# Attention and experts in one kernel: order of the slot scatters, more tiles of the last batch in memory, a fixed first run, independent row scatters and spare banks for transposes

## The chip, the cores and the metric

The kernel runs on one core of a Trainium2 chip. The metric is the device time of one launch in microseconds, a median of several runs. The engines are TensorE (PE, with its weight load PEld), VectorE (DVE), ScalarE (ACT), GpSimd (POOL) and SyncE (SP), which only issues transfers here. Each has a queue of instructions in an order that is fixed when the kernel is built.

## The reference

Two layers with residual additions, on `x` of 4 batches x 1024 tokens x 1024 features and a context of 4 x 1024 x 256, all in float32. The second layer has 8 experts of width 3584, two for each token.

```python
def _L0_xattn_ref(p, k_v, W_k, b_k, ln_gamma, ln_beta):
    kv = k_v @ W_k.T + b_k
    out = jnp.einsum('bij,bjd->bid', p, kv)
    sim = jnp.einsum('bid,bjd->bij', out, kv) * scale
    mu = jnp.mean(sim, axis=-1, keepdims=True)
    var = jnp.var(sim, axis=-1, keepdims=True)
    sim = (sim - mu) * jax.lax.rsqrt(var + EPS) * ln_gamma + ln_beta
    return jax.nn.softmax(sim, axis=-1)

def _L0_ffn_ref(x, gate_w, w1, w2, w3):
    x_flat = x.reshape(-1, d)
    router_probs = jax.nn.softmax(x_flat @ gate_w, axis=-1)
    topk_w, topk_idx = jax.lax.top_k(router_probs, TOP_K)
    topk_w = topk_w / jnp.sum(topk_w, axis=-1, keepdims=True)
...
    h = jax.lax.ragged_dot(x_rep_sort, w1, group_sizes)
    h = jax.nn.silu(h) * jax.lax.ragged_dot(x_rep_sort, w3, group_sizes)
    out_sort = jax.lax.ragged_dot(h, w2, group_sizes)
...
    return jnp.einsum('tkd,tk->td', out_rep, topk_w).reshape(b, s, d)

x = x + _L0_xattn_ref(_layernorm(x), ctx_512, ...)
x = x + _L0_ffn_ref(_layernorm(x), ...)
```

## The kernel before

The kernel has two halves with a hand-over between them.

**Attention, 32 tiles of 128 tokens, 8 per batch.** `front(b)` (L226) prepares a batch: the context is transposed and projected to `kv`, each tile of tokens is loaded (`xt`), normalised (`pn`), transposed into `pT`, and `attend` multiplies with `kv`. `back(b, g)` (L318) then takes one tile: `sim` on PE; its sum of squares on ACT, written over `z`; a power on POOL (`power`, L198: two small operations); the scaling and the softmax on DVE and ACT, in place in `z`; the residual sum `x1`, which SP writes to the output; the layer norm `hn` (`normed`, L206, with one more power on POOL), which SP writes to a scratch tensor `h_d`; eight transposes of `hn`, and eight narrow matmuls for the gate, whose result DVE copies into `lg` (L363). The steps of `front(b + 1)` are put in between the tiles of `back(b, ...)`, so the last batch has none. Pool `wk` gives two buffers to each of `z`, `x1`, `hn` and `pn`, pool `big` two to `pT`.

**Routing.** After each group of four tiles (two groups of two at the end, `GROUPS`) `route` (L368) picks the two experts of each token and its slot in a table `id_d` with a region of `REG` rows for each expert. `put` (L452) scatters token number and weight into the slots: one indirect transfer on POOL for each tile and choice, 64 in all. After every tile two scatters are taken from the list `to_put` (L485), and what is left comes at the end (L500). They are declared independent of one another by the group "puts". The framework places each instruction on its engine's queue by a simulated readiness, program order deciding between those that are ready; an instruction can be pinned behind what was written before it on its engine with `keep_in_program_order`.

**The table of runs.** From the number of tokens of each expert, DVE computes on one partition which expert each run serves (`run_e`), where its slots start (`run_s`), its kind (`run_k`, one of 27 pairs of block count and width in `RUNS`) and how many runs there are (`run_n`), L523 to L584.

**Hand-over.** L926 to L931: `load_rows(first_slot(0))` reads the start of the first run from `run_s`, loads the slots' numbers (`load_ids`, a transfer of SP that waits for all slot scatters), clips them on DVE (`where_from`) and gathers five tiles of rows from `h_d` on POOL. `load_first` loads the first two weight tiles of the expert that `run_e` names. `tokens_in` (L747) transposes the rows into `x`: for each of five tiles, two groups of four transposes into a PSUM tile `pt` of pool `pst`, which has one buffer, and a copy on ACT or DVE.

**Experts.** A loop of two runs a turn (L933), each a `Switch` over the kinds. `run` (L821) works on one or two blocks of up to 564 tokens, with seven products in place of eight (factors are made on DVE). The first part of a block makes the hidden layer (matmuls L855), the second the output (L911). The order of PE is as written here. Small steps are taken from a list `late` between the matmuls: `tokens_out` (L793) transposes results back through `pt`, DVE adds them to the rows, weighted (L802), and after the last quarter POOL scatters each tile of rows to the output (L807); `tokens_in` with `rows_of_out` (L885) prepares the next block and gathers the output's rows. The last quarter of a run is left for the next run (`leftover`, L818), and after the loop for L944. `banks` (L663) takes PSUM for the products: one tile of pool `ps1` and three of pool `ps2`, each of two banks.

Of the kernel before, what the change touches and what calls it, by code (L numbers as in the profile page):

```python
# [9 lines left out]
F32 = mybir.dt.float32  # L10
I32 = mybir.dt.int32
AF = mybir.ActivationFunctionType
ALU = mybir.AluOpType
# [6 lines left out]
P = 128  # L20
N = 512
# [4 lines left out]
MOST = HOLD[-1]  # L26
# [3 lines left out]
TOP_K = 2  # L30
# [4 lines left out]
def kernel(  # L35
# [14 lines left out]
    nc = tc.nc  # L50
    B, S, D = x.shape
# [7 lines left out]
    NT = T // P  # L59
    KM = M // P  # L60
    MAXQ = -(-T // MOST)
    NRUN = (T * TOP_K + E * (MOST - 1)) // MOST
    TAB = 16
    REG = T + -(-(MOST + P) // P) * P
    NONE = 2 * T
# [37 lines left out]
    with ExitStack() as st:  # L103
# [210 lines left out]
                yield lambda h=h: attend(h)  # L314

        lgs = {}

        def back(b, g):  # L318

            row = ts(b * G + g, P)  # L320
            h, i = divmod(g, HG)
            oT, kvT, xt = oTs[b, h], kvTs[b], xts.pop((b, g))
            sim = ps_s.tile([P, J], F32, tag="sim", name="sim")
            for c in range(J // N):
                for d in range(KC):
                    nc.tensor.matmul(
                        sim[:, ts(c, N)], oT[:, d, ts(i, P)], kvT[:, d, ts(c, N)],
                        start=(d == 0), stop=(d == KC - 1),
                    )

            z = wk.tile([P, J], F32, tag="z", name="z")
            ss = sm.tile([P, 1], F32, tag="ss", name="ss")
            nc.scalar.activation(z, sim, AF.Square, accum_out=ss)
            r = power(ss, scale2 / J, SIM_EPS, "s")
            nc.vector.scalar_tensor_tensor(z, sim, r, ngam, ALU.mult, ALU.mult)
            nmax = sm.tile([P, 1], F32, tag="nmax", name="nmax")
            nc.vector.tensor_tensor_reduce(
                z, z, nbet, 1.0, BIG, ALU.add, ALU.min, accum_out=nmax
            )
            den = sm.tile([P, 1], F32, tag="den", name="den")  # L340
            nc.scalar.activation(z, z, AF.Exp, bias=nmax, scale=-1.0, accum_out=den)
            rden = sm.tile([P, 1], F32, tag="rden", name="rden")
            nc.vector.reciprocal(rden, den)
            x1 = wk.tile([P, D], F32, tag="x1", name="x1")
            nc.vector.scalar_tensor_tensor(x1, z, rden, xt, ALU.mult, ALU.add)
            nc.sync.dma_start(out=of[row, :], in_=x1)
            hn = wk.tile([P, D], F32, tag="hn", name="hn")
            normed(hn, x1, "h")
            nc.sync.dma_start(out=h_d[row, :], in_=hn)
            hT = wk.tile([P, KD, P], F32, tag="hT", name="hT")  # L350
            transposed(hT, hn)
            pm = ps_m.tile([P, N], F32, tag="pm", name="pm_g")
            for k in range(KD):
                nc.tensor.matmul(
                    pm[:, :E], hT[:, k, :], gw[:, k, :],
                    start=(k == 0), stop=(k == KD - 1),
                )
            t = b * G + g
            u = max(i for i, (t0, _) in enumerate(GROUPS) if t0 <= t)
            t0 = GROUPS[u][0]  # L360
            if t == t0:
                lgs[u] = wk.tile([P, RG, E], F32, tag="lg", name="lg")
            nc.vector.tensor_copy(lgs[u][:, t - t0, :], pm[:, :E])  # L363
# [4 lines left out]
        def route(u, lg, base):  # L368
# [83 lines left out]
            def put(t, k):  # L452
                to = nc.gpsimd.indirect_dma_start(
                    out=id_d,
                    out_offset=bass.IndirectOffsetOnAxis(ap=pos[:, k, t : t + 1], axis=0),
                    in_=tok[:, k, t, :],
                    in_offset=None,
                )


                if puts:
                    tc.declare_no_dep(to.ins, group="puts", reason="slots are disjoint")
                    for c in cleared:
                        tc.add_manual_dep(to.ins, c.ins.name, SYNC)
                tc.add_to_no_dep_group("puts", to.ins)
                puts.append(to)

            to_put.extend(
# [37 lines left out]
        def row(name, n=E):  # L506
            return tb.tile([1, n], F32, name=name)
# [17 lines left out]
        for j in range(MAXQ):  # L525
            nc.vector.scalar_tensor_tensor(
                nr, n_e, float(j * MOST), nr, ALU.is_gt, ALU.add
            )
        kind, hold = row("kind"), row("hold")
        nc.vector.memset(kind, 0.0)  # L530
        nc.vector.memset(hold, float(HOLD[0]))
# [61 lines left out]
    with ExitStack() as st:  # L593
# [28 lines left out]
        def weights(dst, wf, ex, k0, kn, c0):  # L622
            nc.sync.dma_start(
                out=dst[:, :kn, :],
                in_=wf[ds(ex, 1), :, k0 : k0 + kn, c0 : c0 + QW].rearrange(
                    "e p k m -> (e p) k m"
                ),
            )
# [62 lines left out]
        def expert(i):  # L691
            return nc.values_load(
                run_e[:, ds(i, 1)], engines=(ENG.SP,), min_val=0, max_val=E - 1
            )
# [16 lines left out]
            nc.vector.tensor_scalar(rd, ids[:, :, 0], T - 1, None, ALU.min)  # L711

        def gather(dst, src, rd, s, n):
            nc.gpsimd.indirect_dma_start(
                out=dst,
                out_offset=None,
                in_=src,
                in_offset=bass.IndirectOffsetOnAxis(ap=rd[:n, s : s + 1], axis=0),
            )
# [17 lines left out]
        def load_rows(s0):  # L737
            load_ids(ids0, s0)
            where_from(rd0, ids0)
            for s, r in enumerate(ROWS):  # L740
                gather(rows[s][:r, :], h_d, rd0, s, r)

        def load_first(i, j):

            weights(wts_in[j], (w1f, w3f)[j], expert(i), 0, KD, 0)

        def tokens_in(then=None):  # L747


            def step(s, h):  # L750
                r = ROWS[s]
                pt = pst.tile([P, 4, P], F32, tag="pt", name="pt_h")
                for k in range(HK):
                    nc.tensor.transpose(  # L754
                        pt[:, k, :r], rows[s][:r, ts(HK * h + k, P)], ident[:r, :r]
                    )
                dst = x[:, ds(HK * h, HK), ds(s * P, r)]
                if h % 2:
                    nc.vector.tensor_copy(dst, pt[:, :, :r])
                    if then is not None:  # L760
                        then(s)
                else:
                    nc.scalar.copy(dst, pt[:, :, :r])

            return [lambda s=s, h=h: step(s, h) for s in range(RT) for h in range(2)]
# [24 lines left out]
                p5=v[:, T1, :], p6=t2, p7=t[:, 1, :],  # L790
            )

        def tokens_out(ids, split, q, y):  # L793

            yv = y.rearrange("p (d c) -> p d c", d=2)

            def step(s, r):
                pt = pst.tile([P, 4, P], F32, tag="pt", name="pt_y")
                for d in range(2):
                    nc.tensor.transpose(pt[:r, d, :], yv[:, d, ds(s * P, r)], ident)  # L800
                part = rows[s][:r, ts(q, QW)]
                nc.vector.scalar_tensor_tensor(  # L802
                    part, pt[:r, 0:2, :].rearrange("p a b -> p (a b)"),
                    ids.bitcast(F32)[:r, s, 1:2], part, ALU.mult, ALU.add,
                )
                if q == DQ - 1:
                    nc.gpsimd.indirect_dma_start(  # L807
                        out=of,
                        out_offset=bass.IndirectOffsetOnAxis(ap=ids[:r, s, 0:1], axis=0),
                        in_=rows[s][:r, :],  # L810
                        in_offset=None,
                        bounds_check=T - 1,
                        oob_is_err=False,
                    )

            return [lambda s=s, r=r: step(s, r) for s, r in enumerate(split)]

        def leftover():  # L818
            return tokens_out(ids1, ROWS, DQ - 1, y1)

        def run(i, ex, s0, blocks, width):  # L821
            n = width // 2
# [10 lines left out]
            def take_ids():  # L833
# [3 lines left out]
                nc.vector.tensor_copy(rd, rd0)  # L837
                return ids, rd

            late = leftover()  # L840
            right = token_factors(n)
            for b in range(blocks):
# [41 lines left out]

                def rows_of_out(s):  # L885
                    if s < len(split):
                        gather(rows[s][: split[s], :], of, rd, s, split[s])

                late += tokens_in(rows_of_out)
                if not last:  # L890
# [1 line left out]
                for q in range(DQ):  # L892
                    pp = banks()
                    i2 = 0
                    for u, kn in enumerate(W2K):
# [7 lines left out]
                        if last and q == DQ - 1 and u == len(W2K) - 1:  # L903

                            assert j % WR == WR - 1 == 2
                            load_first(i + 1, 0)
                            load_first(i + 1, 1)
                            late.append(lambda: weight_sums(0, KD, False))
                        hid = [hidden_factors(g[:, i2 + k, :, :], n) for k in range(kn // 2)]
                        for at_m, (p, k) in enumerate(todo):  # L910
# [12 lines left out]
                    late += tokens_out(ids, split, q, y)  # L923
            assert not late

        load_rows(first_slot(0))  # L926
        load_first(0, 0)
        load_first(0, 1)
        for step in tokens_in():
            step()  # L930
        weight_sums(0, KD, False)  # L931
        n_run = nc.values_load(run_n, min_val=2, max_val=NRUN + NRUN % 2)
        with tc.For_i(0, n_run, 2) as i0:  # L933
# [5 lines left out]
            for i, ex, s0, kind, kinds in heads:  # L939
                for k in tc.Switch(kind, kinds):  # L940
                    if k < len(RUNS):
                        with tc.manual_schedule(engines={ENG.PE}):
                            run(i, ex, s0, *RUNS[k])
        for step in leftover():  # L944
            step()


# [26 lines left out]
```

## Time and profile before

| what | us |
|---|---|
| median of three runs | 8915.48 (8914.19 to 8917.11) |
| the profiled execution | 8914.97 |
| its span | 8913.3 |
| first matmul of the experts (L855) | 547.1 |
| last matmul of the experts (L911) ends | 8886.7 |
| mean granted PE clock | 0.988 |

The span runs from the first to the last instruction of one profiled execution. Attention takes about 500 us, routing of the last tiles and the hand-over some 45, the experts the rest. The costliest groups are all matmuls of the experts and their weight loads:

```profile
L855 PE MATMUL ps<-x,w 128*128 128x262 f32 (+5 forms) x10752 | 2482.9, 381 | 45.3 <-issue 34.0
L855 PE MATMUL ps<-xs,s 128*128 128x262 f32 (+5 forms) x7168 | 1628.5, 379 | 5.8 <-DVE xs L772 5.8
L911 PE MATMUL ps<-g,s 128*128 128x262 f32 (+5 forms) x3584 | 1026.0, 379 | 0.0
```

A line names the line of the kernel, the engine, the operation, what it writes and reads, and its count; behind the first bar stand its busy time in us and the mean of one in ns, behind the second the idle time before it and what ended it. POOL is busy for 444.1 us, of which the 64 slot scatters are 70.3 (mean 1.098), the 81 row scatters 103.0 (mean 1.271), the gathers 173.4 and the powers 93.4.

### The profile page before, as it was taken

To read this page: it belongs to the slowest core of one execution; us is meant where nothing else is said; L and a number is where in the kernel's file an instruction comes from. 1 tells how busy PE (TensorE), PEld (TensorE's weight loads), DVE (VectorE), ACT (ScalarE), POOL (GpSimd) and SP (SyncE) were. 2 spreads that over 40 slices of the span, in tenths; PEclk is the share of its full clock that TensorE was granted. 3 is DMA by queue.
4 is the path that set the end of the run, shared out by engine and by line. 5 is a ranking of instruction groups with operands and counts; after the bars stand their busy time and mean duration, and the time that the engine had idled before them with its cause. 6 is when DMAs were issued, how large, how long until landed. Compare 5 with 4: busy or idle time off the path is not lost. (4 is left out here: it accounts for less than half of the span.)

```text
span 8913.3 us, 99092 instructions
## 1 busy us (share of the span) xinstructions
PE 8731.7 (98%) x40738; PEld 7527.1 (84%) x40739; DVE 4824.9 (54%) x8842; ACT 655.3 (7%) x1162; POOL 444.1 (5%) x512
## 2 busy tenths in 40 slices
PE   8979999999999999999999999999999999999998
PEld 5569998999988888888888888888888888888887
DVE  5654645555554545546454554546555464555545
ACT  3310000000000000000000000000000000000000
POOL 2310000000000000000000000000000000000000
PEclk9979999999999999999999999999999999999999
DMA  3222333323232232323323232332323233232322
GB/s 140 110 97 91 107 101 95 110 93 116 92 104 83 88 106 86 110 91 104 98 94 104 90 107 85 101 100 92 109 94 106 83 103 96 90 107 90 106 83 93
DMA packets 769198, 881.77 MB, mean 99 GB/s; under 512 B 33424, under 2 KB 729232, under 8 KB 768608
## 3 DMA queue, kind: packets, MB, share of 16 engines
q1 hardware_dynamic: 734096, 766.12, 26.5%
q0 software_dynamic: 34368, 107.84, 3.6%
q8 instruction: 349, 5.72, 0.3%
q14 instruction: 241, 1.97, 0.1%
q10 hardware_dynamic: 144, 0.13, 0.0%
HBM read 803.61 MB, written 74.87 MB: 99 GB/s over the span
## 5 line engine op out<-in xcount | busy, mean ns | idle before, releaser
L855 PE MATMUL ps<-x,w 128*128 128x262 f32 (+5 forms) x10752 | 2482.9, 381 | 45.3 <-issue 34.0
L855 PEld LDWEIGHTS ps<-x,w 128*128 128x128 f32 x10752 | 2039.9, 190 | 335.0 <-issue 47.4
L855 PE MATMUL ps<-xs,s 128*128 128x262 f32 (+5 forms) x7168 | 1628.5, 379 | 5.8 <-DVE xs L772 5.8
L855 PEld LDWEIGHTS ps<-xs,s 128*128 128x128 f32 x7168 | 1355.7, 189 | 202.5 <-DVE xs L772 7.2
L650 DVE TENSOR_TENSOR s<-w 128x512 f32<-128x512 f32 (+2 forms) x769 | 479.7, 624 | 1602.1 <-DMA w<-in_L_ffn_w_dram 1598.1
L911 PE MATMUL ps<-g,s 128*128 128x262 f32 (+5 forms) x3584 | 1026.0, 379 | 0.0
L911 PE MATMUL ps<-t,w 128*128 128x262 f32 (+5 forms) x3584 | 1024.9, 379 | 0.0
L911 PE MATMUL ps<-g,w 128*128 128x262 f32 (+5 forms) x3584 | 904.6, 381 | 0.0
L855 PE MATMUL ps<-xs,w 128*128 128x262 f32 (+5 forms) x3584 | 848.2, 379 | 0.0
L855 PE MATMUL ps<-x,s 128*128 128x262 f32 (+5 forms) x3584 | 848.2, 380 | 0.0
L689 DVE TENSOR_TENSOR c<-ps,vu 128x524 f32<-128x524 f32 (+5 forms) x448 | 309.9, 692 | 917.8 <-PE ps L855 915.4
L911 PEld LDWEIGHTS ps<-g,s 128*128 128x128 f32 x3584 | 680.1, 190 | 95.1
L855 PEld LDWEIGHTS ps<-x,s 128*128 128x128 f32 x3584 | 680.9, 190 | 94.1
L855 PEld LDWEIGHTS ps<-xs,w 128*128 128x128 f32 x3584 | 678.6, 189 | 96.4
L911 PEld LDWEIGHTS ps<-t,w 128*128 128x128 f32 x3584 | 678.8, 189 | 96.1
L783 DVE TENSOR_TENSOR t<-g 128x262 f32<-128x262 f32 (+5 forms) x896 | 376.4, 425 | 684.6 <-PE ps L911 681.3
L911 PEld LDWEIGHTS ps<-g,w 128*128 128x128 f32 x3584 | 651.4, 190 | 76.6
L784 DVE TENSOR_TENSOR t<-g,t 128x524 f32<-128x524 f32 (+5 forms) x896 | 613.8, 690 | 16.5
L680 ACT COPY p1s<-ps 128x262 f32<-128x262 f32 (+5 forms) x512 | 190.6, 372 | 4666.1 <-PE ps L855 2441.1
L911 PE MATMUL ps<-t,s 128*128 128x262 f32 (+5 forms) x1792 | 512.9, 380 | 0.0
L651 DVE TENSOR_TENSOR s<-s,w 128x512 f32<-128x512 f32 (+2 forms) x769 | 476.3, 619 | 10.1
L652 DVE TENSOR_TENSOR s<-w,s 128x512 f32<-128x512 f32 (+2 forms) x769 | 475.8, 619 | 0.0
(178 smaller groups left out, 4857.2 us busy)
## 6 DMA issues: line engine op xcount, KB each, us to landing
w<-in_L_ffn_w_dram SPq DMA_DIRECT2D x450, 1024.0 KB, 5.0
w<-in_L_ffn_w_dram SPq DMA_DIRECT2D x256, 768.0 KB, 4.4
w<-in_L_ffn_w_dram SPq DMA_DIRECT2D x64, 512.0 KB, 3.5
xt<-in_x_dram SPq DMA_DIRECT2D x32, 512.0 KB, 4.4
out_dram<-x SPq DMA_DIRECT2D x32, 512.0 KB, 2.9
h_d<-hn SPq DMA_DIRECT2D x32, 512.0 KB, 2.6
cx<-in_ctx_dram SPq DMA_DIRECT2D x4, 1024.0 KB, 5.5
id_d<-none SPq DMA_DIRECT2D x5, 512.0 KB, 10.2
```

Source lines behind the costliest of these rows:

```text
L650: nc.vector.tensor_tensor(f["p5"], a21, a22, ALU.add)
L651: nc.vector.tensor_tensor(f["p6"], f["p5"], a11, ALU.subtract)
L652: nc.vector.tensor_tensor(f["p3"], a12, f["p6"], ALU.subtract)
L680: nc.scalar.copy(p1s, one[:, :n])
L689: nc.vector.tensor_tensor(mid, qc[:, :, :n], vu, ALU.add)
L783: nc.vector.tensor_tensor(t2, v[:, B22, :], v[:, T1, :], ALU.subtract)
L784: nc.vector.tensor_tensor(t[:, 1:3, :], v[:, B11 : B21 + 1 : B21 - B11, :], t2.unsqueeze(1).to_broadcast([P, 2, n]), ALU.subtract,)
L855: nc.tensor.matmul(pp[p][:, :n], left[p][:, k, :], right[p][:, k, :], start=(k == 0), stop=(k == HK - 1),)
L911: nc.tensor.matmul(pp[p][:, :n], left[p][:, k, :], hid[k][p], start=(i2 + k == 0), stop=(i2 + k == NI - 1),)
```

## The change

- `put`: each slot scatter is pinned behind what was written before it on POOL.
- `back`, last batch only: `z` is a slice of a `spare` tile of 16 KB a partition, tag `pT`, four to a tile and two such tiles; every second `x1` takes the tag of `z` and every second `hn` that of `pn`.
- First run: expert 0 always has at least one run (`nr` is at least 1), so run 0 is that of expert 0 and starts at slot 0; the first loads take constants instead of the table's entries. `load_first` takes the expert instead of the run. The bound on the number of runs is written anew.
- `tokens_in` before the loop and `leftover` after it take their PSUM tiles from `ps2` (three buffers) instead of `pst` (one).
- Row scatters of one block are declared independent of one another but for the first; the gathers of the output's rows wait for each of them by name.

```diff
-    NRUN = (T * TOP_K + E * (MOST - 1)) // MOST
+    NRUN = (T * TOP_K + E * MOST - (E - 1)) // MOST
...
+        spare = [None]
+        KJ4 = KJ * N // J
...
-            z = wk.tile([P, J], F32, tag="z", name="z")
+            if b == B - 1:
+                if g % KJ4 == 0:
+                    spare[0] = big.tile([P, KJ4, J], F32, tag="pT", name="spare")
+                z = spare[0][:, g % KJ4, :]
+            else:
+                z = wk.tile([P, J], F32, tag="z", name="z")
...
-            x1 = wk.tile([P, D], F32, tag="x1", name="x1")
+            x1 = wk.tile([P, D], F32, tag=("z" if b == B - 1 and g % 2 else "x1"), name="x1")
...
-            hn = wk.tile([P, D], F32, tag="hn", name="hn")
+            hn = wk.tile([P, D], F32, tag=("pn" if b == B - 1 and g % 2 else "hn"), name="hn")
...
                 tc.add_to_no_dep_group("puts", to.ins)
+                tc.keep_in_program_order(to)
...
+        nc.vector.tensor_scalar(nr[:, 0:1], nr[:, 0:1], 1.0, None, ALU.max)
...
-        def load_first(i, j):
-            weights(wts_in[j], (w1f, w3f)[j], expert(i), 0, KD, 0)
+        def load_first(ex, j):
+            weights(wts_in[j], (w1f, w3f)[j], ex, 0, KD, 0)
...
+        def bank(spare, name):
+            if spare:
+                t = ps2.tile([P, 2, N], F32, tag="ps2", name=name)[:, 0, :]
+                return t.rearrange("p (a b) -> p a b", b=P)
+            return pst.tile([P, 4, P], F32, tag="pt", name=name)
...
-                pt = pst.tile([P, 4, P], F32, tag="pt", name="pt_h")
+                pt = bank(spare, "pt_h")
...
+            blocks_sent.append(0)
+            group = f"rows{len(blocks_sent)}"
...
-                pt = pst.tile([P, 4, P], F32, tag="pt", name="pt_y")
+                pt = bank(spare, "pt_y")
...
+                    if s:
+                        tc.declare_no_dep(put.ins, group=group, reason="rows are different")
+                    tc.add_to_no_dep_group(group, put.ins)
+                    sent.append(put)
...
-                        gather(rows[s][: split[s], :], of, rd, s, split[s])
+                        got = gather(rows[s][: split[s], :], of, rd, s, split[s])
+                        for put in sent:
+                            tc.add_manual_dep(got.ins, put.ins.name, SYNC)
+                    if s == RT - 1:
+                        sent.clear()
...
-        load_rows(first_slot(0))
+        load_rows(0)
         load_first(0, 0)
         load_first(0, 1)
-        for step in tokens_in():
+        for step in tokens_in(spare=True):
...
-        for step in leftover():
+        for step in leftover(spare=True):
             step()
```

More of the change, by code (lines that the diff above doesn't have):

```diff
@@ L713, in gather @@
         def gather(dst, src, rd, s, n):
-            nc.gpsimd.indirect_dma_start(
+            return nc.gpsimd.indirect_dma_start(
                 out=dst,
@@ L741, in load_rows, with tokens_in @@
                 gather(rows[s][:r, :], h_d, rd0, s, r)
-        def load_first(i, j):
-            weights(wts_in[j], (w1f, w3f)[j], expert(i), 0, KD, 0)
-        def tokens_in(then=None):
+        def load_first(ex, j):
[5 more added lines that the diff above has]
+            return pst.tile([P, 4, P], F32, tag="pt", name=name)
+        def tokens_in(then=None, spare=False):
             def step(s, h):
                 r = ROWS[s]
-                pt = pst.tile([P, 4, P], F32, tag="pt", name="pt_h")
+                pt = bank(spare, "pt_h")
                 for k in range(HK):
@@ L791, in hidden_factors, with tokens_out @@
             )
-        def tokens_out(ids, split, q, y):
+        sent, blocks_sent = [], []
+        def tokens_out(ids, split, q, y, spare=False):
             yv = y.rearrange("p (d c) -> p d c", d=2)
+            blocks_sent.append(0)
+            group = f"rows{len(blocks_sent)}"
             def step(s, r):
-                pt = pst.tile([P, 4, P], F32, tag="pt", name="pt_y")
+                pt = bank(spare, "pt_y")
                 for d in range(2):
@@ L806, in step @@
                 if q == DQ - 1:
-                    nc.gpsimd.indirect_dma_start(
+                    put = nc.gpsimd.indirect_dma_start(
                         out=of,
@@ L814, in step, with leftover @@
                     )
+                    if s:
+                        tc.declare_no_dep(put.ins, group=group, reason="rows are different")
+                    tc.add_to_no_dep_group(group, put.ins)
+                    sent.append(put)
             return [lambda s=s, r=r: step(s, r) for s, r in enumerate(split)]
-        def leftover():
-            return tokens_out(ids1, ROWS, DQ - 1, y1)
+        def leftover(spare=False):
+            return tokens_out(ids1, ROWS, DQ - 1, y1, spare)
         def run(i, ex, s0, blocks, width):
@@ L886, in rows_of_out @@
                     if s < len(split):
-                        gather(rows[s][: split[s], :], of, rd, s, split[s])
+                        got = gather(rows[s][: split[s], :], of, rd, s, split[s])
+                        for put in sent:
+                            tc.add_manual_dep(got.ins, put.ins.name, SYNC)
+                    if s == RT - 1:
+                        sent.clear()
                 late += tokens_in(rows_of_out)
@@ L905, in run @@
                             assert j % WR == WR - 1 == 2
-                            load_first(i + 1, 0)
-                            load_first(i + 1, 1)
+                            load_first(expert(i + 1), 0)
+                            load_first(expert(i + 1), 1)
                             late.append(lambda: weight_sums(0, KD, False))
```

## The prediction

> **What bounds the kernel now.** I read the page first, then windows by stage, then the waits of the thin stages, then their timelines.
>
> ```profile
> span 8913.3 us, 99092 instructions
> PE 8731.7 (98%) x40738; PEld 7527.1 (84%) x40739; DVE 4824.9 (54%) x8842; ACT 655.3 (7%) x1162; POOL 444.1 (5%) x512
> PE   8979999999999999999999999999999999999998
> PEclk9979999999999999999999999999999999999999
> ...
> 100.00:403.00 303.00, 277.51 (x1251) 174.79 (x1252) 204.11 (x535) 116.11 (x225) 107.32 (x166) 0.94 0.32 115
> 403.00:498.80 95.80, 64.51 (x259) 47.08 (x257) 54.56 (x192) 26.28 (x48) 35.94 (x48) 0.68 0.20 79
> 509.00:560.00 51.00, 23.13 (x95) 18.31 (x96) 19.17 (x38) 5.64 (x8) 4.74 (x5) 0.60 0.35 111
> 560.00:640.00 80.00, 80.00 (x392) 72.85 (x392) 43.48 (x78) 6.63 (x11) 6.28 (x5) 1.00 0.29 93
> 8880.00:8913.30 33.30, 9.12 (x41) 6.44 (x39) 4.95 (x9) 0.00 (x0) 4.89 (x5) 0.68 0.22 85
> ```
>
> PE is idle for 8913.3 - 8731.7 = 181.6 us in all. The expert loop (547 to 8888) is solid matmul but for the starts of runs: its PE waits name 34.0 us of "issue" and 16.4 behind `xs`, of which three loop turns take 10.5 each. The change leaves those alone. So what can be won lies at both ends: columns of the windows are PE, weight loads, DVE, ACT, POOL, then the granted clock. In 403 to 498.8 (the last batch, which has no next batch to fill PE) PE is busy 64.5 of 95.8 us at a clock of 0.68.
>
> ```profile
> DVE lg L363 <- PE pm_g L354: 21.2, 7, 5.3
> DVE hn L213 <- POOL r L203: 10.1, 7, 3.0
> DVE z L335 <- POOL r L203: 6.8, 3, 3.8
> ...
> 502.81 0.96 POOL L453 DMA_INDIRECT id_d<-tok,pos  x1 [0.30 <-issue]
> 511.70 0.16 DVE L569 CAST run_s<-sum_s 1x16 int32<-1x16 f32 x1
> 513.02 0.41 SPq L703 DMA_DIRECT2D ids<-id_d  x1
> 516.21 1.00 POOL L714 DMA_INDIRECT rows<-h_d,rd  x1 [12.45 <-DVE rd L711]
> 524.58 1.09 PE L754 MATMUL pt_h<-ident,rows 128*128 128x128 f32 x4 [27.19 <-DMA rows<-h_d,rd]
> 526.38 1.11 PE L754 MATMUL pt_h<-ident,rows 128*128 128x128 f32 x4 [0.72 <-ACT x L763]
> ...
> 8889.67 1.03 POOL L807 DMA_INDIRECT out_dram<-rows,ids  x1 [144.40 <-DVE rows L802]
> 8893.84 0.99 POOL L807 DMA_INDIRECT out_dram<-rows,ids  x1 [3.14 <-DVE rows L802]
> 8906.13 0.92 POOL L807 DMA_INDIRECT out_dram<-rows,ids  x1 [3.13 <-DMA out_dram<-rows,ids]
> ```
>
> First three lines: what DVE waits for in the last batch (total, times, longest). Then the hand-over to the experts: the last slot scatter has left at 503.8, yet the load of `ids` starts at 513.0, 1.2 us after the cast of `run_s`, the start of the first run. The first rows land 8.3 us after their gather starts, beside three weight loads of 1 MB whose packets move at up to 410 GB/s. Then each of ten groups of transposes waits for the copy of the one before: one every 1.85 us. At the end the five row scatters go one per 4.1 us, each behind the landing of the last.
>
> **The change, part by part** (against the profiled execution: 8914.97 us, 0.5 under the median of the three runs, 8915.48; span 8913.3).
>
> *Row scatters independent, three banks at the end.* Scatters whose order is free are seen in the slot scatters: one per 1.26 us (0.96 + 0.30). Five rows scatters then start at 8889.67 + 4 x 1.26 = 8894.7 at the latest, not 8906.13: **-11.4**. Is POOL or the transfer next? A full scatter is 0.5 MB and its packets took 1.3 us at up to 424 GB/s, just the issue interval, so no queue builds up. Rows must be ready by then: DVE L802 of the last tile ends at 8893.64 today, and with three banks it is DVE's 0.48 five times from 8888.9, 8891.4. I take -11.3; ends -8 (each scatter at the 2 us that the longest row scatter took, 1.95) and -11.5. The cover of the last scatter, 6.25 us from its issue to the end of the span, stays.
>
> *Three banks for the first transposes.* PE needs 8 x 1.10 + 2 x 0.69 = 10.2 us, copies alternate between ACT (0.58) and DVE (0.69) and fit beside. Today it is 524.58 to 541.64 = 17.1. With the last copy 0.42: **-6.5**. If the rows landed slower than 2.2 us per tile, that would be next; five gathers leave at 1.26 intervals.
>
> On the clock: these transposes ran at a granted 0.50 while 59% busy, and in the first run the matmuls go from 0.31 to 0.23 us each after 4.8 us without a gap. The Trainium skill (TensorE: Matmul & The Clock Gate, "Part 1: The HAM clock gate") states that the full clock returns after about 3.4 us of sustained work; by it the second half of the closer-set transposes would take half the time, and the sum would be some 3 us lower. The row at hand agrees on the return, not on whether 128-column transposes are dense enough.
>
> *First run fixed.* `load_rows(0)` needs the slot scatters, no longer the table. Scatter out at 503.8, landing 3.1 (the row scatters' wait for a landing), so `ids` leaves at 506.9, arrives 2.1 later (513.02 to 515.16): 509.0. What is late next is DVE's queue: the table's small operations fill it without a gap until 511.9, and `rd` (L711) stands behind or between them. I place it behind: 512.0, gather at 513.0 (today 516.2). The weights of expert 0 depend on nothing in the table any more and can run earlier than 513.7, so the gathers share the transfer engines with one weight load, not three. A landing alone is 0.94 + 3.1 = 4.1, beside three loads 8.3: I take 6, so rows at 519.0 rather than 524.5: **-5.5**. Ends: 0 (weights still beside, `rd` late) and -10 (`rd` at 509.2, landing in 4.1). The 5.5 us from the last copy to the first matmul (547.14) is entry into the loop and stays. The rewritten number of runs is 17208/1128 and 17209/1128, both 15; the floor of 1 on `nr` is one operation of 0.15 us in DVE's table, off the path once `ids` does not wait for it.
>
> *Slot scatters in written order.* No operation is added; two follow each tile's own powers instead of eight in a row. Today in batches 0 to 2 a power stands behind them, and PE pays:
>
> ```profile
> 218.64 0.96 POOL L453 DMA_INDIRECT id_d<-tok,pos  x1 [0.30 <-issue]
> 219.67 0.19 POOL L201 TENSOR_SCALAR v<-ss 128x1 f32<-128x1 f32 x1
> 221.88 6.45 PE L326 MATMUL sim<-kvT,oT 128*128 128x512 f32 x10 [6.67 <-DVE z L335]
> ```
>
> The sum of squares was there at 215.0, the power began at 219.7. The same 6.7 us gap is at 330.9. With two scatters ahead at most (2.5 us) each gap shrinks by 2 to 4.7; the ten matmuls behind took 6.45 instead of 10 x 0.46 (24 in 10.95 at 406.5) because the clock had dropped, 1.9 more each. **-8** for both; ends -17 (both gaps and dips gone) and +7 (one more such gap: a pinned scatter that waits for its `pos` holds the powers behind it on POOL, which stood still for 12.8 us before the one at 480.4).
>
> Against this part speaks a rule. Slot scatters took 0.95 to 1.99 us, and the long ones (166.9, 320.7) lie over a TENSOR_SCALAR that writes `pn`. The Trainium skill (SBUF — State Buffer, the "DVE blocks DMA" trap) states that some DVE passes lock GpSimd out while it writes a transfer's descriptors. The trace agrees in those two places. Written order puts a scatter just behind the power that releases `hn` (0.81 on DVE); by the rule the first of each pair costs 1 us more, and this term would be -6.
>
> *More tiles of the last batch under way.* `z` gets eight places, `x1` and `hn` four. Ends: DVE was busy 54.6 of the 95.8 us, and the closing chain from `hn` at 484.9 to the last `pos` at 498.8 is serial, 13.9; 54.6 + 13.9 = 68.5 gives -27. On the other side the waits at `lg` (21.2) may grow by half: +11. Directly named are ACT's waits for a free `z`, 3.8 us in three, and the two waits for POOL behind scatters, 3.0 and 3.8. Their sum is 10.6; not all is on the path: **-8**.
>
> Memory for the extra tiles is that of `pT`, free since 403, and tags idle in this batch. Inside the loop, scatters are 12.6 us apart, so their freedom buys nothing there; each gather of output rows now waits for up to five scatters by name, but these landed some 300 us before: 0.
>
> Sum: -11.3 - 6.5 - 5.5 - 8 - 8 = -39.3, so 8914.97 - 39.3 = **8876 us**.
>
> **Rivals.**
> 1. *The last batch comes to DVE's pace.* For: four to eight tiles under way, DVE idle for 41 us. Against: its order is set before the run, and the 21.2 us at `lg` come from PE at half clock, not from places. 19 more: 8857.
> 2. *The attention stage only reshuffles.* The queue orders change, waits move, nothing is won. For: PE's waits in 460 to 500 are a dependent chain. Then only the hand-over and the end count, -23.3: 8892.
> 3. *Slower: DVE's queue in the last batch.* With twice the tiles under way, passes of other tiles stand ahead of those PE needs. Today 7 waits at `lg` cost 3.0 each. If both `hn` and `z` of each of eight tiles came to wait as long, it is 8 x 2 x 3.0 = 48, and the sum is 8915 - 23 + 48 = 8940. It decides once the batch loses more than 23 us. Against: the first tiles stay first in priority, and places only take waits away.
> 4. *It does not do what it says.* The scatters stay chained through the output tensor, or `ids` still comes behind the table: without the 11.3 and some of the rest, 8887 to 8892.
>
> **How the numbers follow.** Forecast 0.62 (own range 8862 to 8890), rival 1 0.14, rival 2 0.14, rival 4 0.05, rival 3 0.05. What a measurement can tell from no change is 0.2%, 17.8 us: faster means below 8897.6. Forecast and rival 1 are faster, of rival 2 0.08 and of rival 4 0.03: 0.87; the rest of these two is 0.08 within; rival 3 is 0.05 slower. The range, 8852 to 8902, takes in most of rivals 1, 2 and 4 and leaves rival 3 out.
>
> **What would show it.** Five row scatters 1.26 us apart at the end, and 12 us from the first of them to the end of the span instead of 23.6; transposes of the first rows back to back, 10 us long; `ids` issued before the cast of `run_s`; the two 6.7 us waits of `sim` gone, no more than two slot scatters between powers; the last batch under 90 us. The prediction is wrong if the stage from 403 to the last `pos` grows, if the first rows still land 8 us after their gather, or if waits in the loop exceed 55 us.

## The result and the profile after

Five runs each on one chip: the changed kernel 8878.57 us (8871.27 to 8880.48), the kernel before 8915.63 (8914.19 to 8918.31). The ratio, estimated from the runs and not the quotient of the two medians, is 0.9955, 95% interval [0.9943, 0.9967]. By the medians the change is 37 us faster, against 39 forecast (8876). The profiled execution took 8878.68 us, its span is 8876.9.

Two lines of the page of the changed kernel:

```profile
span 8876.9 us, 99078 instructions
PE 8731.2 (98%) x40738; PEld 7527.9 (85%) x40739; DVE 4822.1 (54%) x8843; ACT 655.0 (7%) x1162; POOL 448.8 (5%) x512
```

PE does the same work (8731.2 us busy, 8731.7 before); its idle time fell from 181.6 to 145.7. So the gain is idle time of PE at the two ends. The timelines give marks that cut the span into pieces; each number below is the difference of two starts or ends in a timeline.

| piece (us) | before | after | won | forecast |
|---|---|---|---|---|
| start to the end of the last `attend` matmul | 403.2 | 395.0 | 8.2 | 8 (written order) |
| to the last cast of `pos` (last batch) | 95.6 | 90.5 | 5.1 | 8 (tiles) |
| to the first transpose of gathered rows | 25.8 | 18.8 | 7.0 | 5.5 |
| to the last copy into `x` | 17.1 | 10.4 | 6.7 | 6.5 |
| to the first expert matmul | 5.5 | 4.9 | 0.6 | 0 |
| to the end of the last expert matmul | 8339.6 | 8342.0 | -2.4 | 0 |
| to the end of the span | 26.6 | 15.3 | 11.3 | 11.3 |

Each column is one profiled execution. In further executions with the same queues, shown below, the second piece is up to 3.7 us longer, and the first and the fourth differ by up to 2.

The hand-over in the timeline of the changed kernel (start, duration, engine, line, what is written and read):

```profile
490.96 0.96 POOL L462 DMA_INDIRECT id_d<-tok,pos  x1 [0.30 <-issue]
493.19 0.38 SPq L714 DMA_DIRECT2D ids<-id_d  x1
493.63 1.15 SPq L634 DMA_DIRECT2D w<-in_L_ffn_w_dram  x2
498.10 0.14 DVE L722 TENSOR_SCALAR rd<-ids 128x5 int32<-128x5 int32 x1
499.21 1.00 POOL L725 DMA_INDIRECT rows<-h_d,rd  x1 [7.30 <-DMA w<-in_L_ffn_w_dram]
500.01 0.19 DVE L580 CAST run_s<-sum_s 1x16 int32<-1x16 f32 x1
504.40 3.27 PE L772 MATMUL pt_h<-ident,rows 128*128 128x128 f32 x16 [20.44 <-DMA rows<-h_d,rd]
508.97 1.07 PE L772 MATMUL pt_h<-ident,rows 128*128 128x128 f32 x8 [1.30 <-DMA rows<-h_d,rd]
511.31 2.99 PE L772 MATMUL pt_h<-ident,rows 128*128 128x128 f32 x16 [1.27 <-DMA rows<-h_d,rd]
519.60 5.83 PE L884 MATMUL ps<-x,w 128*128 128x246 f32 x16 [5.31 <-issue]
```

`ids` now leaves 1.3 us after the last slot scatter has gone out, 6.8 before the cast of `run_s` that it used to follow. The transposes stand in blocks of 16 and 8; what parts them is no copy any more, but rows that have not landed.

The end, where each row scatter used to start 4.1 us after the last:

```profile
8864.53 1.03 POOL L829 DMA_INDIRECT out_dram<-rows,ids  x1 [144.39 <-DVE rows L824]
8865.87 0.99 POOL L829 DMA_INDIRECT out_dram<-rows,ids  x1 [0.31 <-DVE rows L824]
8869.73 0.92 POOL L829 DMA_INDIRECT out_dram<-rows,ids  x1 [0.30 <-issue]
```

### The profile page after: what moved, and what is told of

It reads as the page before. It is cut to its first block, busy times and chain, and to the rows that moved or that the text cites. A ratio compares the mean times of both kernels' runs of the same rounds, so it can differ in the third digit from the quotient of the medians.

```text
span 8876.9 us, 99078 instructions
## 1 busy us (share of the span) xinstructions
PE 8731.2 (98%) x40738; PEld 7527.9 (85%) x40739; DVE 4822.1 (54%) x8843; ACT 655.0 (7%) x1162; POOL 448.8 (5%) x512
## 5 line engine op out<-in xcount | busy, mean ns | idle before, releaser
L944 PEld LDWEIGHTS ps<-g,s 128*128 128x128 f32 x3584 | 680.1, 190 | 95.1
L884 PEld LDWEIGHTS ps<-x,s 128*128 128x128 f32 x3584 | 680.9, 190 | 94.1
## 6 DMA issues: line engine op xcount, KB each, us to landing
id_d<-none SPq DMA_DIRECT2D x5, 512.0 KB, 10.4
```

What stands on the lines that cost most here:

```text
L884: nc.tensor.matmul(pp[p][:, :n], left[p][:, k, :], right[p][:, k, :], start=(k == 0), stop=(k == HK - 1),)
L944: nc.tensor.matmul(pp[p][:, :n], left[p][:, k, :], hid[k][p], start=(i2 + k == 0), stop=(i2 + k == NI - 1),)
```

## The experiments

Eleven runs, each beside runs of the kernel before on its own chip. Behind each median stands the estimated ratio to that, with its 95% interval. The intervals of most single parts overlap that of the changed kernel, so it is the pieces of the traces, more than the times, that tell what a part is worth. Undoing a part of the changed kernel should give back that part's piece.

**Without the pin** (`u_order`):

```diff
-                tc.keep_in_program_order(to)
```

> The changed kernel without the pin on the slot scatters. Marks of the changed kernel: last matmul of attend ends at 395.0, last cast of pos at 485.6, first rows transposed from 504.4. Theory (written order won the 8.2 us in batches 0 to 2, the tiles won the 5.0 in the last batch): attend ends at about 403 again with the two 6.7 us waits of sim back, the last batch keeps its 90.5 us, so the total is 8 above the changed kernel, 8887. Rival 1 (written order also won the last batch): the last batch takes 95 or more, 8892. Rival 2 (the order of the queues moved by chance, the pin is not the cause): attend ends at 395 to 398, 8879 to 8882.

8887.91 us, 0.9969 [0.9956, 0.9981]. The last `attend` ends at 405.9, the last cast of `pos` is at 496.9, 11.3 later than in the changed kernel, 10.9 of it in batches 0 to 2 (last batch 90.9). PE's waits for DVE's `z` in attention, first without the pin (to 405 us), then the changed kernel (to 403); columns are total, times and longest:

```profile
PE sim L329 <- DVE z L344: 13.3, 2, 6.7
```

```profile
PE sim L329 <- DVE z L344: 6.2, 2, 3.1
```

The two gaps are the same two places, cut from 6.7 to 3.1 each. The theory holds; the second rival, chance, falls. It falls by the other traces too. With the pin the last `attend` ends at 391.0 to 397.6 in all nine, and from 60 us to that mark PE idles for 20.7 to 22.4 us. Without it, in four, the mark is at 403.1 to 405.9 and the idle time 29.2 to 29.3.

**Without the extra tiles** (`u_tiles`):

```diff
-            if b == B - 1:
+            if False:
...
-            x1 = wk.tile([P, D], F32, tag=("z" if b == B - 1 and g % 2 else "x1"), name="x1")
-            hn = wk.tile([P, D], F32, tag=("pn" if b == B - 1 and g % 2 else "hn"), name="hn")
+            x1 = wk.tile([P, D], F32, tag="x1", name="x1")
+            hn = wk.tile([P, D], F32, tag="hn", name="hn")
```

> The changed kernel with z, x1 and hn of the last batch as before (two buffers each). Theory: batches 0 to 2 do not change (attend ends at 395), the last batch from there to the last cast of pos takes 95.6 us again instead of 90.5, total 8884. Rival 1 (the last batch's gain is that of written order alone): it stays at 90 to 91, 8879. Rival 2 (the tiles gain more, but the order gives it back): 100 or more without them, 8889.

8880.61 us, 0.9962 [0.9948, 0.9976]. The last batch takes 95.1, as the theory has it, but the last `attend` ends at 391.0, four earlier, so the last `pos` is at 486.1: half a microsecond from the changed kernel's 485.6. The four are no work that the tiles move across the mark: from 60 us to it PE runs 1388 matmuls here and 1390 in the changed kernel, and idles for 21.2 and 21.3 us. It is busy for 309.8 us here and 313.8 there, at a granted clock of 0.96 and 0.95. Whether that comes from the tiles or from the execution, one trace cannot tell. The split of the two pieces in the table is therefore no measure of the two parts; only their sum is.

The waits that the tiles were to take away, for powers of POOL and for a free `z`, are all still here with the pin in place (the last batch, 391 to 486.1):

```profile
DVE hn L214 <- POOL r L204: 9.5, 7, 3.0
DVE z L344 <- POOL r L204: 6.2, 3, 3.2
ACT z L342 <- DVE x L354: 3.8, 3, 1.8
```

In the kernel before they were 10.1, 6.8 and 3.8. With the tiles as well, in the control further below, the first two are 5.3 and 3.7 and the third is gone: 10.5 us of waits less, and the last `pos` no earlier.

**The first run from the table again** (`u_first`):

```diff
-        load_rows(0)
-        load_first(0, 0)
-        load_first(0, 1)
+        load_rows(first_slot(0))
+        load_first(expert(0), 0)
+        load_first(expert(0), 1)
```

> The changed kernel with the first loads taken from the table again (start of the run and expert read from it). Theory: ids leaves 1.2 us after the cast of run_s, which ends some 13 us after the last cast of pos; from the last cast of pos to the first transpose 25 to 26 us instead of 18.8, total 7 above, 8886. Rival (the landing beside the weights is what counts, and it is the same either way): the gather starts 3 us later only and lands as fast, 8881 to 8882.

8884.98 us, 0.9965 [0.9952, 0.9977]. From the last `pos` to the first transpose 26.3 us, 7.5 more, as expected. But the transposes take only 7.6, so 2.8 comes back. The timeline and two windows of this kernel (columns PE, weight loads, DVE, ACT, POOL, then the granted clock, the mean busy share of the DMA engines and GB/s):

```profile
516.51 7.15 PE L772 MATMUL pt_h<-ident,rows 128*128 128x128 f32 x40 [29.08 <-DMA rows<-h_d,rd]
```

```profile
516.50:521.50 5.00, 4.99 (x24) 4.96 (x24) 1.38 (x2) 1.62 (x3) 0.00 (x0) 0.50 1.06 309
521.60:523.60 2.00, 1.89 (x18) 1.46 (x16) 1.29 (x2) 0.80 (x3) 0.00 (x0) 1.00 0.94 294
```

Here all rows come before PE needs them, forty transposes run without a gap, and the clock rises from 0.50 to 1.00 some 5 us after the first. The earlier start of the changed kernel meets the landing of the rows instead: part of what the first edit wins, the second loses.

**One bank again** (`u_banks`): `spare=False` at both calls.

> The changed kernel with one bank for the transposes before and after the loop. Theory: transposes of the first rows take 17 us instead of 10.35, total 6.7 above, and nothing is lost at the end, because rows are ready 1.02 us apart with one bank and POOL needs 1.3 for a scatter: 8885. Rival (the banks are part of the tail's gain): 2 to 4 us more at the end, 8888.

8886.41 us, 0.9965 [0.9953, 0.9978]. Transposes 17.2 us; the end 15.3 as with three banks. The theory holds on both counts; the banks are no part of the tail.

**Row scatters dependent again** (`u_rows`):

```diff
-                    if s:
-                        tc.declare_no_dep(put.ins, group=group, reason="rows are different")
-                    tc.add_to_no_dep_group(group, put.ins)
```

> The changed kernel with the row scatters left dependent through the output tensor; three banks stay. Theory: the five scatters at the end stand 4.1 us apart again, from the last expert matmul to the end of the span 26.6 us instead of 15.3, total 11.3 above the changed kernel, 8890. Rival (part of the tail is the banks): 24 to 25 us, 8888.

8891.08 us, 0.9972 [0.996, 0.9983]. From the last expert matmul to the end 26.9 us, 11.6 more. The second and the last of the five scatters of this kernel:

```profile
8870.22 0.99 POOL L829 DMA_INDIRECT out_dram<-rows,ids  x1 [3.14 <-DMA out_dram<-rows,ids]
8882.52 0.92 POOL L829 DMA_INDIRECT out_dram<-rows,ids  x1 [3.13 <-DMA out_dram<-rows,ids]
```

Both name the landing of the scatter before as what they waited for. The whole tail is the dependence.

**The tiles alone, in the kernel before** (`b_tiles`; the edit of `back` and nothing else):

> The kernel before with the tiles of the last batch alone (z in spare, second tags for x1 and hn); the slot scatters float as before. Theory (the tiles are worth about 2 us by themselves, because places were not what the last batch waited for): 8913 to 8915, the same as before. Rival 1 (they are worth the 8 us of the prediction, and written order hides it): 8907. Rival 2 (more tiles under way and floating scatters hurt each other): 8918 or more.

8911.04 us, 0.9995 [0.9986, 1.0004], unclear by time, though the median is 6.6 under that of before on this chip. The one trace agrees with the median: the last `attend` ends at 403.1 as before, the last batch takes 89.8 instead of 95.6. Between theory and first rival: some 6 us when the scatters float.

**Neither pin nor tiles, beside a control** (`u_both`, both edits above undone; `control`, the changed kernel itself):

> The changed kernel itself, on the chip of the two next to it, as their common measure; 8876 to 8881, and its last cast of pos between 484 and 490, where five executions with the same queues stood.

> The changed kernel with neither the pin nor the tiles. It closes the square of the two: without the pin alone the last cast of pos stood at 496.9, without the tiles alone at 486.1, with both the control's. Theory (written order carries it; the tiles help only where scatters float): pos at 499, as in the kernel before, total 11 to 13 above the control. Rival (the two add): 14 to 18 above the control.

The control: 8883.06 us, 0.9957 [0.9944, 0.9971], last `pos` at 491.0, outside the expected bands by two and by one. Without both: 8896.15, 0.9975 [0.9966, 0.9985], last `pos` at 499.1. The difference of the medians is 13.1 us, just above the theory's 11 to 13 and below the rival's 14 to 18; that of these two traces at `pos` is 8.1. The square, by the last cast of `pos`:

| | no pin | pin |
|---|---|---|
| two buffers | 499.1 (before: 498.8) | 486.1 |
| more tiles | 496.9 (`b_tiles`: 492.9) | 485.6, 491.0, and 490.2, 488.4, 486.4, 490.2 in `u_first`, `u_banks`, `u_rows`, `i_weights` |

The last cell is one set of queues up to there, in six executions; they scatter over 5.4 us, so a difference of 2 or 3 between cells says nothing. What stands above it: the pin is worth 13.0 with two buffers, from one trace each; the tiles some 2 to 6 without the pin, and with it nothing that can be seen (mean of the six 488.6, against 486.1). The medians, each against the kernel before on its chip, agree: 36.3 us under it without the tiles, 37.1 and 35.3 with them.

**The gate's copy on ACT in the last batch** (`i_lg`, and `i_lg_again` beside the control):

```diff
-            nc.vector.tensor_copy(lgs[u][:, t - t0, :], pm[:, :E])
+            (nc.scalar.copy if b == B - 1 else nc.vector.tensor_copy)(lgs[u][:, t - t0, :], pm[:, :E])
```

> The changed kernel with the copy of the gate's result into lg on ACT instead of DVE, in the last batch only. Theory (DVE's queue stands at these copies for some 20 us, and what stands behind them is late): the last batch gets 5 to 10 us shorter, 8869 to 8874. Rival 1 (the last batch is a chain through PE at half clock, whoever copies): 8877 to 8880. Rival 2 (ACT's queue now stands instead and holds back squares and exponentials): 8882 or more.

> The changed kernel with the gate's copy on ACT in the last batch, once more beside the control. Theory (the queue of DVE at these copies is worth a few us): 3 us under the control, pos 3 earlier. Rival (that was the scatter from one execution to the next): within 1 us of the control.

8875.29 us, 0.9955 [0.9939, 0.997], last batch 88.5, between the theory and the first rival; then 8877.82, 0.9954 [0.994, 0.9967], last batch 87.7, against 8883.06 and 94.1 of the control. Both medians are 3 to 5 under the changed kernel, but the intervals cover one another: whether it is faster stays open. What DVE waits for in the last batch, first the control (397 to 491), then `i_lg_again` (397 to 486):

```profile
DVE lg L372 <- PE pm_g L363: 22.9, 7, 5.3
DVE hn L214 <- POOL r L204: 5.3, 6, 2.4
DVE spare L344 <- POOL r L204: 3.7, 3, 2.6
```

```profile
DVE spare L344 <- POOL r L204: 13.2, 4, 5.7
DVE lmax L390 <- ACT lg L372: 6.6, 2, 3.4
DVE hn L214 <- POOL r L204: 4.1, 7, 0.7
```

The 22.9 us at `lg` are gone, and most of it has turned into waits for the powers and for ACT. That speaks for a chain rather than a crowded queue, but does not prove it.

**Weights ahead of `ids`** (`i_weights`):

```diff
-        load_rows(0)
         load_first(0, 0)
         load_first(0, 1)
+        load_rows(0)
```

> The changed kernel with the first two weight loads written ahead of the load of ids, so that SP need not wait for the slot scatters before it issues them. Theory (weight loads beside the gathers delay the later rows: two waits of 1.3 us between the transposes): the weights are in before the gathers start, the transposes take 7.6 to 9 us instead of 10.35, and 2 to 3 us are won, 8876. Rival (the third weight load, inside the loop, is what they meet): no change, 8878 to 8879.

8882.98 us, 0.9961 [0.9945, 0.9976]: the expected 8876 was missed; the control has 8883.06, so by time nothing changed. The trace shows two reasons.

```profile
496.40 1.01 SPq L634 DMA_DIRECT2D w<-in_L_ffn_w_dram  x2
497.46 1.04 SPq L714 DMA_DIRECT2D ids<-id_d  x1
```

The last slot scatter had gone out at 495.1; the weights leave 1.3 us later, just when `ids` would have. They wait for the slot scatters too, and ahead of `ids` they only hold it up by 1.1 us and share the way with it: `rd` waits for `ids` until 7.9 us after its issue (2.0 from issue to landing in the changed kernel) and comes 10.2 us behind the last scatter, against 6.2 in the changed kernel and 8.4 in the control. The theory itself fails as well. Both weight tiles had landed by 504.7, before the first gather left at 506.5, and PE still waits for rows between the transposes, once for 2.25 us; they take 11.1. So these two loads are not what holds up the later rows. The rival's third load, issued at 507.2, stays possible and was not tested.

## Why the prediction was right, point by point

The hand-over and the end came out by the mechanisms forecast. That the total came within some 2 us is partly luck: the pin brought more than its term, the tiles less, and the sum for the banks has two errors that cancel.

- *Row scatters*: forecast -11.3, 11.3 in the table, 11.6 given back by `u_rows`. The reading of the slot scatters (one per 1.26 us when free) carried over: 1.28 to 1.34.
- *Banks*: forecast -6.5, 6.7 measured, 6.8 given back by `u_banks`. The mechanism was right: no block of transposes waits for a copy in this trace. The exact size is luck: set closer, the transposes keep PE busy for 7.3 us, not 10.2, and 2.6 us of waiting for rows, which the sum put at nothing, nearly make that up. In the nine traces with three banks and `ids` ahead of the table the piece took 10.0 to 12.3 us, against 17.1 to 17.2 with one bank.
- *The note on the clock*: `u_first` settles that 128-column transposes without gaps bring the clock back, some 5 us after the first. In the changed kernel it was 0.50 from 504.4 to 507.1, 1.00 from 507.2 to 510.5, and 0.50 again behind that, so a part of this gain is in its 7.3 us. The Trainium skill (TensorE: Matmul & The Clock Gate, "Part 1: The HAM clock gate") gives about 3.4 us of sustained work; 5.1 us in the one and 2.7 in the other lie on both sides of it. The prediction's 4.8 us for the first run is the length of a merged row: in that trace the clock was 0.50 up to 549.9 and 1.00 from 550.1, 3 us after the first matmul.
- *First run*: forecast -5.5, 7.0 measured. `rd` stands behind DVE's table, as placed (498.1, five after `ids` left), 3.8 us sooner behind `pos` than before, where 3.2 was forecast. The first transpose begins 5.2 us after the gather, 6 assumed. Wrong in it: a landing of 3.1 before `ids` could go, which was 1.3. The weights go right behind `ids`, and in `i_weights`, where they are written ahead of it, they left no sooner after the slot scatters.
- *Slot scatters*: forecast -8, bounds -17 and +7; 13.0 by the square. Up to the end of `attend` that pair of traces (`u_both` and `u_tiles`) differs by 12.5: 8.1 us of PE's idle time, and 4.4 of its busy time, at a clock of 0.95 and 0.96. The mechanism was right (gaps of 6.7 cut to 3.1), the size too small. Two of its signs did not come: the gaps are not gone, and six scatters still stand in a row between two powers (168.4 to 177.3).
- *More tiles*: forecast -8; alone 2 to 6, on top of the pin nothing visible, and the last batch took 90.5 to 94.2 us in the six executions, not under 90. This is the term that was mis-sized, in the step "Their sum is 10.6; not all is on the path": the tiles took 10.5 us of waits of these three kinds away, yet next to the pin none of it shows at the last `pos`. The pin had not taken them before, as `u_tiles` shows. Other waits grew instead: from `u_tiles` to the control, DVE's at `lg` from 21.1 to 26.1, and PE's for `mask` from 4.2 to 10.9. Why the tiles help when the scatters float stays open. The two terms together, forecast 16, measured 13.2 in the profiled pair and 13.1 in time (`u_both` against the control).
- *Rivals*: DVE's pace in the last batch (68.5 us) is far from 88 to 94; the reshuffle without gain, the slower queue and the change without effect are refuted by the pieces.
- *The rule against the pin*: slot scatters took 1.130 us on the mean instead of 1.098, not 1 us more for each first of a pair. Those at 390.4 and 444.3, each begun just after an `hn` pass, took 1.59; those at 414.4 and 452.8, begun likewise, 1.06. The Trainium skill (SBUF — State Buffer, the "DVE blocks DMA" trap) is borne out only in part, and the price of 2 us that the prediction drew from it for this term is not to be seen.

## What to carry to other kernels

Where transfers write different places and the program cannot see it, the chain that their order makes is read off the trace directly: the interval with the landing as its releaser, against the interval of the same kind of transfer declared free. A wait that an edit takes away is time won only where it stands on the path: the tiles removed 10.5 us of named waits, and the last mark of the stage stayed where it was. And in a chain through several in-order queues, take a part's gain at a mark behind the chain and from several executions: such a mark stood up to 5.4 us apart here with the same queues.

## What was not expected

Six executions with the same queues up to the last cast of `pos` had it between 485.6 and 491.0 us, while the expert loop's 8340 us differed by 5 in all kernels (8338.4 to 8343.7). Of the 7.5 us between the spans of the changed kernel and its control, 5.4 lie ahead of that cast. The granted clock, which changes between 0.50 and 1.00 there, does not explain it alone: in the window of 435 to 455 us it was 0.50 in the control and 0.67 in `u_rows`, but 0.50 also in the changed kernel, whose cast came first of all. What makes the scatter stays open.
